# Attention and mixture-of-experts kernel, second phase: another order of the filling work on TensorE

## The chip, the cores and the metric

The kernel runs on one core of one Trainium2 chip. The metric is device time in microseconds (us), as a median of repeated executions. Beside them one execution was taken by the hardware profiler; all durations of single instructions come from it. Five engines work side by side, each in the order of its own queue: TensorE (PE, with weight loads listed apart as PEld), VectorE (DVE), ScalarE (ACT), GpSimd (POOL) and SyncE (SP, which only starts transfers here).

## The reference

The input has 8 rows of 1024 positions with 256 features. Three stages follow one another:

1. An attention within each position over the 64 channels of each of 16 heads, a projection back, a residual and a layer norm.
2. A multi-head attention with 4 heads of 64. Here the first axis (8) is the sequence and the second (1024) the batch, so each position attends over the 8 rows. Then an output projection, a residual and a layer norm, which gives `y1`.
3. A mixture of 8 experts with a capacity, chosen by the largest gate, a residual and two layer norms.

The part that matters for this change is stage 2 and the gates of stage 3:

```python
q, k, v = jnp.split(x @ w.T + b, 3, axis=-1)            # x: (8, 1024, 256)
scores = jnp.einsum('nhld,nhmd->nhlm', q, k) / sqrt(64)  # l, m over the 8 rows
o = jnp.einsum('nhlm,nhmd->nhld', softmax(scores), v)
y1 = ln(x + o @ ow.T + ob) * ln1_g + ln1_b
gates = softmax(y1 @ wg)                                 # 8 experts
```

## The kernel before

The program has three phases, one for each stage. The change lies in the second, `phase_b`.

**Groups.** The 1024 positions are cut into 8 groups of 128. A group `j` holds 128 positions of all 8 rows, 1024 tokens. For the attention the tokens of a group are rearranged into 8 blocks of 128 tokens: 16 positions with their 8 rows each. A block's scores are one 128x128 product, and a bias of -1e30 hides pairs of different positions.

**Steps.** A group is worked in four steps `n` (called parts here). Step `n` treats the feature half `c = n // 2` (two of the four heads) and four blocks, half `ib = n % 2`. Its own work is: `scores` on TensorE with a row maximum on DVE, `weights` (8 exponentials on ACT, in two halves of four), and `normed` on DVE. The step after that transposes the weights (`turn_s` on TensorE, a copy to `sT` on ACT) and multiplies them by the values (`weighted` on TensorE, a copy to `oT` on ACT). So the step before is always completed inside the current one.

**Filling work.** Between these, each step runs a list of filling work written by hand in `fills(j)`. It holds work for the next group (`nxt = j + 1`: `turn_x` transposes its input, `project_qk` and `project_v` make queries, keys and values) and for the group before (`prv = j - 1`: `output`, `normal`, `turn_y`, `logits`, `exps`, `choice`). `put(part, condition, function, arguments)` appends a job to the list of a part. The order of emission is the order in each engine's queue, because the scheduler is switched off (`manual_schedule`): an instruction that waits holds up everything behind it on its engine. The loop places the jobs so: one job after `scores` and before the first four exponentials; two jobs between `turn_s` and the last four exponentials; the rest after `weighted`. In part 0, `some` stops in front of an `output`, as that needs `oT` of the step before.

**What each job puts where.** A pair means two of the 8 rows; `l0` is 0, 2, 4 or 6.

- `turn_x(j, l0)`: four transposes on TensorE, two copies to `xT` on DVE. There is one `xT` buffer. The four calls together fill it, and each `project_qk` reads all rows of it.
- `project_qk(j, c, which, half)`: four 512-wide products on TensorE, one bias on ACT. `which` is 0 for queries and 1 for keys, `half` picks four of the eight blocks. The last one, `(1, 1, 1)`, is first read by the scores of part 3.
- `project_v(j, b0)`: eight products, one addition on DVE.
- `output(j, l0)`: first `xb`, the input plus a bias, on POOL (line 732); four products on TensorE; the sum `r` on DVE (line 750), which reads both; then moments on DVE and the inverse root on POOL (lines 69 to 75).
- `normal(j, l0)`: two scalings on DVE (line 759), a multiplication and an addition on POOL (line 762) that finish `y`, a third operation on POOL (line 763), and a store by SP.
- `turn_y(j, l0)`: four transposes of `y` on TensorE (line 774), a copy to `yT` on ACT.
- `logits(j, l0)`: eight small products on TensorE (line 786), a copy on DVE.
- `expert_bias`: two operations on DVE, over a weight tile that SP loads.

**PSUM.** All filling jobs and `weighted` take their PSUM tile from one pool of three, named `fill`; the scores have a pool of two double tiles, and one tile belongs to the experts:

```python
tc.tile_pool(name="bsc", bufs=2, space=PSUM) as p2,
tc.tile_pool(name="bps", bufs=1, space=PSUM) as p1,
tc.tile_pool(name="bfill", bufs=3, space=PSUM) as pf,
```

The loop that sets where jobs stand among the step's own work:

```python
st = scores(j, c, ib)
some(1)
weights(st, 0)
...
sT = turn_s(before[3])
some(2 if live else 0)
...
weighted(*before[:3], sT)
...
some(len(work))
```

Group `j = -1` only prepares group 0, group 7 has no next group (two experts are computed there instead, as filling), and `j = 8` completes group 7.

Of the kernel before, what the change touches and what calls it, by code (L numbers as in the profile page):

```python
# [38 lines left out]
L, N = 8, 1024  # L39
NT = L * N // P  # L40
NJ = N // P
# [4 lines left out]
EARLY = 2  # L46
# [494 lines left out]
def phase_b(tc, a, ident, x1_d, rows_d, keep, norm_scalars):  # L541
# [8 lines left out]
    with (  # L550
# [315 lines left out]
        def fills(j):  # L866


            o = [[], [], [], []]
            nxt, prv = j + 1, j - 1  # L870
            N = nxt < NJ
            O = prv >= 0
            X = 0 <= j < E - EARLY

            def put(part, ok, fn, *args):
                if ok:
                    o[part].append((fn, *args))

            put(0, N, turn_x, nxt, 0)
            put(0, N, turn_x, nxt, 2)  # L880
            put(0, N, turn_x, nxt, 4)
            put(0, O, output, prv, 0)
            put(0, N, turn_x, nxt, 6)
            put(0, O, output, prv, 2)
            put(0, X, expert_bias, EARLY + j, 0)
            put(0, O, normal, prv, 0)
            put(0, N, project_qk, nxt, 0, 0, 0)
            put(1, O, normal, prv, 2)
            put(1, O, turn_y, prv, 0)
            put(1, O, output, prv, 4)  # L890
            put(1, N, project_qk, nxt, 0, 0, 1)
            put(1, O, logits, prv, 0)
            put(1, O, normal, prv, 4)
            put(1, O, turn_y, prv, 2)
            put(1, X, expert_bias, EARLY + j, 1)
            put(1, N, project_v, nxt, 0)
            put(1, O, logits, prv, 2)
            put(1, N, project_qk, nxt, 0, 1, 0)
            put(2, O, turn_y, prv, 4)
            put(2, O, output, prv, 6)  # L900
            put(2, N, project_qk, nxt, 0, 1, 1)
            put(2, O, logits, prv, 4)
            put(2, O, normal, prv, 6)
            put(2, X, expert_bias, EARLY + j, 2)
            put(2, N, project_v, nxt, 2)
            put(2, N, project_qk, nxt, 1, 0, 0)
            put(2, N, project_v, nxt, 4)
            put(3, O, turn_y, prv, 6)
            put(3, N, project_qk, nxt, 1, 0, 1)
            put(3, N, project_v, nxt, 6)  # L910
            put(3, O, logits, prv, 6)
            put(3, O, exps, prv)
            put(3, X, expert_bias, EARLY + j, 3)
            put(3, N, project_qk, nxt, 1, 1, 0)
            put(3, O, choice, prv)
            put(3, N, project_qk, nxt, 1, 1, 1)
            if j == NJ - 1:
                for n in range(4):
                    for i in range(EARLY):
                        k = EARLY * n + i  # L920
                        put(n, True, expert, *divmod(k, 4))
            return o

        before = None
        for j in range(-1, NJ + 1):
            if j < 0:
                load_x(0)
                load_x(1)
            parts = fills(j)
            for n in range(4):  # L930
                work = list(parts[n])
# [454 lines left out]
```

## Time and profile before

| What | Value |
|---|---|
| Time, median of 3 (lowest to highest) | 5169.2 us (5164.46 to 5169.56) |
| The profiled execution's own time | 5132.98 us |
| Its span, first to last instruction | 5131.2 us |
| Mean granted TensorE clock | 0.980 |
| First phase, up to the first `turn_x` wait's end | 0 to 4356.4 us |
| Group -1 and group 0 of the second phase | 4356.4 to 4426.1 us |
| Groups 1 to 6 | 4426.1 to 4775.9 us |
| Groups 7 and 8 | 4775.9 to 4886.3 us |
| Third phase | 4886.3 to 5131.2 us |

The starts of groups 1 to 7, taken at the first matmul of their scores (line 660), are 4426.11, 4483.68, 4543.64, 4601.84, 4659.94, 4718.00 and 4775.87 us. A group thus takes about 58 us, of 5131 in all. Times in the text are read on this axis; "start to start" is the distance between the first instructions of two neighbouring runs of matmuls on TensorE, because the ends of matmuls are modelled and overlap the next start. A wait in brackets behind an instruction is the idle time of its engine before it and what ended it.

### The profile page before, as it was taken

To read this page: it belongs to the slowest core of one execution; us is meant where nothing else is said; L and a number is where in the kernel's file an instruction comes from. 1 tells how busy PE (TensorE), PEld (TensorE's weight loads), DVE (VectorE), ACT (ScalarE), POOL (GpSimd) and SP (SyncE) were. 2 spreads that over 40 slices of the span, in tenths; PEclk is the share of its full clock that TensorE was granted. 3 is DMA by queue.
4 is the path that set the end of the run, shared out by engine and by line. 5 is a ranking of instruction groups with operands and counts; after the bars stand their busy time and mean duration, and the time that the engine had idled before them with its cause. 6 is when DMAs were issued, how large, how long until landed. Compare 5 with 4: busy or idle time off the path is not lost. (4 is left out here: it accounts for less than half of the span.)

```text
span 5131.2 us, 189707 instructions
## 1 busy us (share of the span) xinstructions
PE 4902.1 (96%) x79688; PEld 3308.8 (64%) x79688; DVE 3068.7 (60%) x6088; ACT 3359.7 (65%) x4123; POOL 3369.5 (66%) x7014
## 2 busy tenths in 40 slices
PE   7999999999999999999999999999999997888775
PEld 4666666666666666666666666666666664566563
DVE  5656656666666666566665666666566663455467
ACT  4777777777777777777777777777777774444334
POOL 5676676767776676776776776776767675245446
PEclk9999999999999999999999999999999998999897
DMA  2222222222221222222222222222222222122253
GB/s 75 47 48 48 48 47 48 49 47 48 48 49 46 48 48 48 49 49 46 48 49 46 49 49 46 48 49 46 48 48 47 48 49 67 47 67 73 70 185 115
DMA packets 575501, 286.30 MB, mean 56 GB/s; under 512 B 395057, under 2 KB 526257, under 8 KB 574641
## 3 DMA queue, kind: packets, MB, share of 16 engines
q1 hardware_dynamic: 366162, 111.51, 11.0%
q0 software_dynamic: 204800, 159.82, 10.5%
q8 instruction: 623, 10.21, 0.9%
q10 hardware_dynamic: 3680, 2.83, 0.2%
q14 instruction: 236, 1.93, 0.1%
HBM read 72.31 MB, written 33.59 MB: 21 GB/s over the span
## 5 line engine op out<-in xcount | busy, mean ns | idle before, releaser
L359 ACT ACTIVATE e<-pair 128x1024 f32<-128x1024 f32 x3072 | 2977.4, 1021 | 1241.5 <-PE pair L343 1241.5
L403 POOL DMA_DIRECT2D nd<-S x4096 | 1949.3, 484 | 603.6 <-DVE S L393 410.1
L343 PE MATMUL pair<-R,L 32*128 32x128 f32 (+1 forms) x32768 | 1607.0, 323 | 3.8 <-POOL event L314 3.7
L393 DVE COPY S<-sum 128x512 f32<-128x512 f32 x1024 | 706.9, 690 | 1470.3 <-PE sum L382 1143.5
L343 PEld LDWEIGHTS pair<-R,L 32*128 32x128 f32 x32768 | 1271.8, 186 | 50.7 <-POOL event L314 5.0
L373 PE MATMUL sum<-e,V 128*32 128x256 f32 x16384 | 1285.8, 385 | 4.9 <-DVE S L393 4.9
L300 POOL DMA_DIRECT2D R<-qm x2048 | 973.7, 483 | 78.0 <-issue 39.5
L382 PE MATMUL sum<-e,V 128*32 128x128 f32 x16384 | 823.8, 273 | 0.0
L382 PEld LDWEIGHTS sum<-e,V 128*32 128x32 f32 x16384 | 533.1, 110 | 352.8 <-issue 1.8
L373 PEld LDWEIGHTS sum<-e,V 128*32 128x32 f32 x16384 | 406.5, 109 | 236.8 <-DVE vT L241 41.8
L331 PE MATMUL pair<-late,sel 32*128 32x256 bf16 (+1 forms) x6144 | 499.3, 313 | 9.6 <-ACT e L359 9.6
L254 DVE COPY V<-vT 32x128 f32<-32x128 f32 x2048 | 457.5, 223 | 28.1
L331 PEld LDWEIGHTS <-sel 32*128 32x128 bf16 x6144 | 155.4, 91 | 460.6 <-issue 445.2
L412 DVE RECIPROCAL att<-nd 128x256 f32<-128x256 f32 x256 | 447.4, 1747 | 7.2 <-DMA nd<-S 3.3
L314 POOL MEMSET event<- 1x1 f32 x256 | 22.6, 88 | 627.1 <-DMA R<-qm 419.7
L223 PE MATMUL ps<-wk,xT 128*128 128x512 f32 x512 | 257.6, 626 | 10.8 <-DMA wk<-in_Wk 10.0
L234 PEld LDWEIGHTS ps<-xT,wv 128*128 128x128 f32 x2048 | 238.2, 191 | 45.1 <-issue 41.8
L234 PE MATMUL ps<-xT,wv 128*128 128x128 f32 x2048 | 262.6, 281 | 1.6 <-DVE qm L267 0.8
L266 PE MATMUL ps<-wq,xT 128*128 128x512 f32 x512 | 257.5, 626 | 6.5 <-DVE k L224 6.5
L443 PE MATMUL ps<-wo,attT 128*128 128x256 f32 x1024 | 256.9, 394 | 0.7 <-ACT attT L426 0.7
L443 PEld LDWEIGHTS ps<-wo,attT 128*128 128x128 f32 x1024 | 185.4, 191 | 63.3 <-issue 41.8
L73 POOL TENSOR_SCALAR ve<-mv 128x1 f32<-128x1 f32 x128 | 37.4, 292 | 270.2 <-DVE mv L71 268.7
(191 smaller groups left out, 3841.3 us busy)
## 6 DMA issues: line engine op xcount, KB each, us to landing
R<-qm POOLq DMA_DIRECT2D x2048, 32.0 KB, 2.1
nd<-S POOLq DMA_DIRECT2D x4096, 16.0 KB, 1.9
L<-k SPq DMA_DIRECT2D x4088, 8.0 KB
rows_d<-yx SPq DMA_DIRECT2D x32, 512.0 KB
xT<-in_xT SPq DMA_DIRECT2D x64, 128.0 KB
xr<-in_x SPq DMA_DIRECT2D x64, 128.0 KB
x_d<-x1o SPq DMA_DIRECT2D x64, 128.0 KB
x<-x_d SPq DMA_DIRECT2D x8, 1024.0 KB
```

The costliest lines, as they stand in the source:

```text
L234: nc.tensor.matmul(ps[:, i * P : (i + 1) * P], w["v"][:, c, ch * P : (ch + 1) * P], xT_of[t][:, c, :], start=c == 0, stop=c == DC - 1,)
L254: nc.vector.tensor_copy(V[32 * aa : 32 * aa + 32, qd % 2, :, qd // 2, :, aa, 0:4], src[32 * qd : 32 * qd + 32, :, ww, :, aa, :],)
L300: moved.append((None, nc.gpsimd.dma_start(R[:, b, s, b, :], q[:, b, s, cols])))
L331: nc.tensor.matmul(bank[u].rearrange("p (n i) -> p n i", i=n)[:, :, 0:32], sel[pr].rearrange("p a j -> p (a j)"), late[pr, None, :].to_bro ...
L343: one = nc.tensor.matmul(bank[u][:, x * 4 * n : (x + 1) * 4 * n].rearrange("p (b i) -> p b i", i=n), Lt[pr, 2 * (h0 + h) + jb].rearrange(" ...
L359: nc.scalar.activation(e, pair[i], AF.Exp)
L373: nc.tensor.matmul(dst[32 * u : 32 * u + 32], Vs[ww][:, 0, h0 + h, u, :], e0[u // 2][:, u % 2, x * 256 : (x + 1) * 256].rearrange("p (b i) ...
L382: nc.tensor.matmul(dst[32 * u : 32 * u + 32, :, 32:], Vs[ww][:, 1, h0 + h, u, :], e1[u // 2][:, u % 2, h * 128 : (h + 1) * 128].rearrange( ...
L393: nc.vector.tensor_copy(S[:, :, 2 * which : 2 * which + 2, :].rearrange("p b h i -> p h b i"), ps.rearrange("p (h b i) -> p h b i", h=2, b=4),
L403: nc.gpsimd.dma_start(tok[:, b, s, h0 * C1 : (h0 + G) * C1], Sx[:, 4 if s else b, b, :])
L412: nc.vector.reciprocal(att[:, cols], nd[:, 1, cols])
L443: nc.tensor.matmul(ps[:, :D], attT[:, c, :], wo[:, c, :], start=c == 0, stop=c == HID // P - 1)
```

## The change

The lists of `fills` are put in another order; no job is added or taken away.

```diff
+            put(0, 0 < j < NJ, project_qk, j, 1, 1, 1)
             put(0, N, turn_x, nxt, 0)
...
             put(0, N, project_qk, nxt, 0, 0, 0)
+            put(1, N, project_qk, nxt, 0, 0, 1)
             put(1, O, normal, prv, 2)
+            put(1, O, output, prv, 4)
             put(1, O, turn_y, prv, 0)
-            put(1, O, output, prv, 4)
-            put(1, N, project_qk, nxt, 0, 0, 1)
+            put(1, X, expert_bias, EARLY + j, 1)
+            put(1, N, project_v, nxt, 0)
             put(1, O, logits, prv, 0)
             put(1, O, normal, prv, 4)
             put(1, O, turn_y, prv, 2)
-            put(1, X, expert_bias, EARLY + j, 1)
-            put(1, N, project_v, nxt, 0)
+            put(1, N, project_qk, nxt, 0, 1, 0)
             put(1, O, logits, prv, 2)
-            put(1, N, project_qk, nxt, 0, 1, 0)
...
-            put(3, N, project_qk, nxt, 1, 1, 1)
+            put(3, j < 0, project_qk, nxt, 1, 1, 1)
```

In part 1, the job between the scores and the exponentials was `normal` of pair 2 and is now a projection. The two behind `turn_s` were `turn_y` of pair 0 and `output` of pair 4 and are now `normal` of pair 2 and `output` of pair 4. `turn_y` of pair 0 comes after `weighted`, followed by `expert_bias` and `project_v`, then `logits` of pair 0. The last projection of a group (keys, second feature half, blocks 4 to 7) leaves part 3 of the group before and becomes the first job of part 0 of its own group, between the scores and the exponentials. For group 0 it stays where it was. In part 0 `turn_x` of pairs 0 and 2 then stand behind `turn_s`, and that of pair 4 behind `weighted`.

## The prediction

> **What bounds the kernel now.** I read three views in this order: the busy time by stretch (to find the second phase and its limit), TensorE's waits in that stretch, then the order of time of each engine for one group of eight rows. The page's busy line and the stretch of groups 1 to 6 come first:
>
> ```profile
> PE 4902.1 (96%) x79688; PEld 3308.8 (64%) x79688; DVE 3068.7 (60%) x6088; ACT 3359.7 (65%) x4123; POOL 3369.5 (66%) x7014
> ...
> 4426.10:4775.90 349.80, 311.25 (x1971) 224.39 (x1972) 206.25 (x460) 152.48 (x510) 165.22 (x192) 0.94 0.27 69
> ```
>
> The columns are the stretch, its length, then busy time of PE, PEld, DVE, ACT and POOL, the granted clock, DMA share and GB/s. TensorE is busy 311 of 350 us there, so it sets the pace; its gaps are all there is to win. The waits of TensorE in this stretch, all of them:
>
> ```profile
> PE fill L774 <- POOL yx L762: 23.2, 6, 3.9
> PE fill L717 <- ACT sT L707: 10.8, 6, 2.1
> PE fill L623 <- DVE xT L612: 3.8, 6, 0.6
> PE fill L742 <- ACT oT L725: 0.8, 5, 0.2
> ```
>
> One wait a group, 3.9 us, for y of the first pair, and one of 1.8 us for sT in part 0. The order of time on TensorE, group 4, part 1 (start, length, engine, line; in brackets the idle time before):
>
> ```profile
> 4616.52 1.09 PE L705 MATMUL sc<-ident,s 128*128 128x128 f32 x8
> 4621.54 1.12 PE L774 MATMUL fill<-ident,yx 128*128 128x128 f32 x4 [3.93 <-POOL yx L762]
> 4622.45 3.62 PE L742 MATMUL fill<-wout,oT 128*128 128x256 f32 x8
> 4626.00 1.41 PE L717 MATMUL fill<-sT,v 128*64 128x128 f32 x16
> 4627.34 1.98 PE L623 MATMUL fill<-xT,wi 128*128 128x512 f32 x4
> 4629.16 0.95 PE L786 MATMUL fill<-wg,yT 128*128 128x8 f32 x8
> ```
>
> After the 3.93 us gap the output product takes 3.55 us from start to start, against 1.73 us in parts 0 and 2. From 4621.54 to 4627.34, 5.80 us hold work that elsewhere takes 0.48 + 1.73 + 1.03 = 3.24. So each such gap costs a further 2.56 us; over groups 1 to 6 this extra is 1.8, 2.8, 2.6, 2.6, 2.5, 2.7, mean 2.5. The chain behind the gap lies on POOL and DVE, same group:
>
> ```profile
> 4620.10 1.39 POOL L762 TENSOR_TENSOR yx<-yx,row_ln_b 128x512 f32<-128x512 f32 x1
> ...
> 4626.51 1.27 POOL L732 TENSOR_TENSOR xb<-x,row_out_b 128x512 f32<-128x512 f32 x1
> ...
> 4627.81 0.69 DVE L750 TENSOR_TENSOR r<-fill,xb 128x512 f32<-128x512 f32 x1 [6.18 <-POOL xb L732]
> ```
>
> y of pair 0 is there at 4621.49. POOL then runs the rest of normal 0, all of normal 2 and only then xb of pair 4, so DVE empties the output product of pair 4 at 4628.50. That last time is the one to keep in mind. Where it already bites is seen in group 7, which has no projections as filling:
>
> ```profile
> 4805.68 0.66 PE L774 MATMUL fill<-ident,yx 128*128 128x128 f32 x4 [1.97 <-DVE r L750]
> ```
>
> Transposes of y have nothing to do with r; what they wait for is the PSUM buffer. The "fill" pool has three; in that part the order is turn_y 0, output 4, weighted, logits 0, turn_y 2, and the fifth waits for the second to be emptied. Buffers go round by three.
>
> **The Trainium skill.** "TensorE: Matmul & The Clock Gate", Part 1, "What's actually happening", says that the array falls to half rate after an idle window and needs about 3.4 us of activity, in a free-running window, to come back. The trace agrees in kind (1.73 becomes 3.55 us); gaps of 1.73 us left the rate alone in five groups, one of 2.13 us (group 2, part 0) did not. "PSUM — Partial Sum Buffer", "Specifications (TRN2)": 8 banks of 512 fp32 values. Pools here take 2x2 (sc) + 1 (pw) + 3 (fill) = 8, so no fourth fill buffer exists. "Perfetto Trace Analysis", "Optimization Strategy": the same gap repeated on the saturated engine can mean that buffers ran out; L774 in group 7 shows just that.
>
> **The change, part by part**, in group 4 (T0 = 4601.84, T1 = 4615.31, T2 = 4634.87 are the starts of parts 0, 1, 2).
>
> *Part 1 reordered.* Nothing is added or removed. New order with TensorE's warm lengths: scores 1.21 (to 4616.52), project_qk 1.82 (18.34), turn_s 0.87 (19.21), output 4 1.73 (20.94), weighted. It waits for sT, which ACT finishes at 4621.55 + 1.02 = 22.57: the row max on DVE, which it hangs on, stays behind the norm of pair 0. ACT does the projection's bias (0.69) before the exponentials, with time to spare. Gap 1.6 us, then weighted to 23.6 and turn_y 0 to 24.1, whose y has been there since 21.49: that wait is gone. Next in TensorE's queue stands project_v 0. Fill buffers now: project_qk, output 4, weighted, turn_y 0, project_v 0. The fifth needs the second empty: r of pair 4, 4628.50. Before, the fifth was logits 0, reached at 4629.16, 0.66 us after the buffer was free; the change puts TensorE there 4.4 us before. Behind the stall wait logits 0, turn_y 2, project_qk and logits 2; all later work follows. POOL's order is unchanged, so 4628.50 does not move by itself.
>
> After it: 1.73 (v) + 0.81 + 0.48 + 1.82 + 0.81 = 5.65 us warm, 0.06 for the release, and the slow rate after a gap of over 3.9 us, 2.5. T2 = 28.50 + 0.06 + 5.65 + 2.5 = 36.71 against 34.87: +1.84. Bounds of the slow rate: 1.0 (a lucky phase) to 2.8, so +0.3 to +2.1. The expert bias and v on DVE change places; the norm of pair 4 comes some 2 us later, so POOL has y of pair 4 near 4637.2; turn_y 4 asks at T2 + 1.21 = 37.9: covered, by 0.7. SP's stores and weight loads keep their order. Six groups: 6 x 1.84 = +11.0.
>
> *Projection held back.* Part 3 is shorter by 1.8 us, part 0 longer by it. It stands ahead of turn_s, and turn_x 4 goes behind weighted. TensorE reaches weighted at T0 - 1.8 + 1.21 + 1.82 + 0.87 + 0.9 = T0 + 3.0; sT came at T0 + 5.34. Whether sT moves up depends on what the row max waits for:
>
> ```profile
> 4603.17 1.23 DVE L680 TENSOR_REDUCE mx<-sc 128x8 f32<-128x1024 f32 x1 [0.54 <-PE sc L671]
> ```
>
> In group 4 it waits 0.54 us for the scores after the choice ended on DVE, so 0.5 us is won. In groups 2, 3 and 5 the max starts as the choice ends (a weight load is late before it), so nothing; group 6 gains 0.25, group 1 (no choice, then bound by the bias of the projection on ACT) 0.7. Sum -1.45. So the moved projection mostly fills the gap it opened. But the gap before weighted becomes 1.5, 2.7, 2.3, 1.8, 2.3, 2.1 us in groups 1 to 6. Group 2, slow before, shows the price of crossing:
>
> ```profile
> 4489.43 1.32 PE L717 MATMUL fill<-sT,v 128*64 128x128 f32 x16 [2.13 <-ACT sT L707]
> 4490.68 3.40 PE L742 MATMUL fill<-wout,oT 128*128 128x256 f32 x8
> ```
>
> There r of pair 0 came 1.2 us later after weighted than in other groups (4.76 against 3.56), and the POOL chain starts there. I count groups 3 and 5 and half of 6: 2.5 x 1.2 = +3.0, between 0 and 6.
>
> *Groups 7 and 8.* In 7, part 0 has its gap cut from 3.04 to 2.35 and everything 0.85 earlier; in part 1 logits 0 becomes the fourth fill and waits for r of pair 4, so logits 0 (0.8 warm, 1.4 slow) stands behind 4805.63 - 0.85 as well as turn_y 2 and logits 2. Net +0.5, between -1 and +2. In 8 output 4 goes under the 8.7 us wait for y, but POOL's chain sets that part's end: 0.
>
> Sum: 11.0 - 1.45 + 3.0 + 0.5 = +13 us. The profiled execution took 5132.98 (span 5131.2): 5146. The timed runs have a median of 5169.2, 36 us above; I carry the difference over unchanged: 5182.
>
> **Rivals.** *Forecast, stall moves to the buffer of output 4*: 5182, own range 5171 to 5190. For it: L774 above, waiting for r. *Faster*: buffers do not bind, only the wait for y goes. Then each group saves 3.93 + 2.55 less the new 1.6 before weighted, 4.9 us, six times 29: 5140. Against it: three buffers and the wait in group 7; it would need POOL to reach xb of pair 4 about 4.4 us sooner, and its order is not touched. It decides as soon as r of pair 4 is out before 4624.1. Chance 0.11. *Near nothing*: the stall is there but the slow rate costs about 1 us, and held-back gaps stay warm: 6 x 0.3 - 1.45 + 0.5, about +1, 5170; with middling values up to 5179. Chance 0.22 for this stretch. *Worse*: all six part-0 gaps go slow and part 1 costs 2.1: 12.6 - 1.45 + 7.2 + 2 = +20: 5189. Chance 0.14. The forecast proper has 0.53.
>
> 0.2% of the time, 10.3 us, is what I take as measurable, so slower begins at 5179.5. The forecast (about 0.47 of its 0.53) and worse give slower 0.61; near nothing and the low edge of the forecast 0.27; faster 0.12 (its rival, and a far edge of near nothing). Range: from 5165 to 5193; it leaves out the faster rival and the ends.
>
> **What would show it.** TensorE's waits for yx gone in groups 1 to 6; in their place project_v (L641) waiting 4.4 us for DVE r L750, six times, and double lengths after it; weighted waiting about 1.6 us more in part 1. Part 0 gaps as listed. I am wrong if L641 does not wait, or if r of pair 4 is emptied before turn_y 0 ends.

## The result, and the profile after

The changed kernel takes 5197.32 us (median of 4, 5194.19 to 5200.45) where the kernel before takes 5166.83 (median of 4, 5157.26 to 5169.56): ratio 1.0059, 95% interval 1.0046 to 1.0073, or 30 us more. The direction was forecast; the size was 2.3 times the 13 us of the sum, and the time lies above the range.

The profiled execution of the changed kernel has a span of 5192.5 us, 61 above that of the kernel before, and 40 of these have nothing to do with the change. The busy time by stretch of the changed kernel shows it (columns as in the prediction; groups 1 to 6, then the third phase):

```profile
4418.87:4796.14 377.27, 325.07 (x1970) 234.44 (x1970) 200.62 (x454) 150.67 (x510) 163.97 (x192) 0.91 0.25 64
...
4907.70:5192.50 284.80, 176.80 (x712) 128.68 (x712) 180.99 (x510) 102.97 (x240) 135.93 (x191) 0.79 0.43 133
```

The third phase, untouched, takes 284.8 us here and 244.9 in the profile before. Both lengths recur below whatever the kernel: 243 to 245 in all profiles from chips where the kernel before takes 5128, 288 in the one from a chip where it takes 5171. What makes the chips differ is not shown. This phase is left out of comparisons of two profiles. The second phase, from the first `turn_x` to the first matmul of the third phase, grew from 529.3 us (4357.05 to 4886.33) to 556.2 (4351.49 to 4907.68): +26.9, close to the measured 30. Groups 1 to 6 carry it, 349.8 before and 377.3 after, at a granted clock of 0.91 against 0.94.

TensorE's waits in groups 1 to 6 of the changed kernel (line, what it waited for, total, times, longest):

```profile
PE fill L641 <- DVE r L750: 25.7, 6, 4.3
PE fill L717 <- ACT sT L707: 19.5, 12, 2.3
PE fill L623 <- DVE xT L612: 3.7, 6, 0.6
PE fill L623 <- ACT yT L778: 3.4, 5, 0.7
```

The wait for y (23.2 us before) is gone, and `project_v` waits for the sum r of pair 4 instead, 4.3 us six times. Line 717, `weighted`, now waits twice a group. The last line was not foreseen. Part 1 of group 3 in order of time, first on TensorE, then the one line of DVE that ends the stall:

```profile
4569.61 1.09 PE L717 MATMUL fill<-sT,v 128*64 128x128 f32 x16 [1.50 <-ACT sT L707]
4570.64 0.66 PE L774 MATMUL fill<-ident,yx 128*128 128x128 f32 x4
4575.56 3.78 PE L641 MATMUL fill<-wi,xT 128*128 128x256 f32 x8 [4.27 <-DVE r L750]
4579.14 1.71 PE L786 MATMUL fill<-wg,yT 128*128 128x8 f32 x8
4580.70 1.09 PE L774 MATMUL fill<-ident,yx 128*128 128x128 f32 x4
4582.47 3.78 PE L623 MATMUL fill<-xT,wi 128*128 128x512 f32 x4 [0.68 <-ACT yT L778]
4586.05 1.44 PE L786 MATMUL fill<-wg,yT 128*128 128x8 f32 x8
```

```profile
4574.82 0.69 DVE L750 TENSOR_TENSOR r<-fill,xb 128x512 f32<-128x512 f32 x1 [6.17 <-POOL xb L732]
```

The transposes of y (L774) start at once behind `weighted`. The stall comes next, and ends as DVE empties the buffer of `output` 4 (4574.82 + 0.69 = 4575.51). Then look at the lengths: `project_v` 3.58 us start to start instead of 1.73, the logits 1.56 instead of 0.81, the projection 3.58 instead of 1.82. The half rate lasts from 4575.56 until after 4586, about 11 us; in the kernel before it lasted about 5.

The granted clock, the column behind the five busy times, says the same without any lengths of matmuls. Two stretches of the changed kernel (groups 3 and 4), then one of the kernel before (group 4):

```profile
4573.40:4587.06 13.66, 10.82 (x30) 7.62 (x30) 5.50 (x13) 1.27 (x2) 8.79 (x10) 0.50 0.16 60
4638.26:4641.67 3.41, 2.88 (x7) 2.35 (x8) 3.27 (x8) 0.00 (x0) 2.01 (x4) 0.50 0.25 92
```

```profile
4619.85:4626.68 6.83, 5.14 (x18) 3.96 (x20) 1.79 (x3) 4.41 (x18) 6.67 (x7) 0.50 0.41 107
```

In groups 1 to 6 of both profiles, and of those of all experiments below, the granted clock is either 1.00 or 0.50, and it changes only at times that lie whole multiples of 3.41 us apart, on a grid that lies elsewhere in every run. So the half rate comes in whole pieces of 3.41 us. Counted by the part in which they begin, part 1 of groups 1 to 6 has 1, 2, 2, 2, 2 and 2 pieces in the kernel before and 3, 4, 4, 1, 5 and 3 in the changed one, whose part 1 is shortest (21.31 us) in group 4 with one piece and longest (25.38) in group 5 with five.

Part lengths over groups 1 to 6, from the starts of the scores:

| | Before | After |
|---|---|---|
| Part 0 | 13.46 to 13.48 (15.08 in group 2) | 14.39 to 15.03 (16.79 in group 2) |
| Part 1 | 19.04 to 19.81, sum 116.9 | 21.31 to 25.38, sum 143.6 |
| Part 2 | 13.40 | 13.40, in two groups 14.8 |
| Part 3 | 11.67 | 9.95 |

### The profile page after: what moved, and what is told of

Its sections match the earlier page's. It is cut to its first block, busy times and chain, and to the rows that moved or that the text cites. A ratio compares the mean times of both kernels' runs of the same rounds, so it can differ in the third digit from the quotient of the medians.

```text
span 5192.5 us, 189702 instructions
## 1 busy us (share of the span) xinstructions
PE 4922.2 (95%) x79688; PEld 3323.9 (64%) x79688; DVE 3064.0 (59%) x6088; ACT 3358.0 (65%) x4123; POOL 3370.5 (65%) x7014
```

## The experiments

Each time stands beside runs of the kernel before on the same chip; its median was 5128.3 to 5128.9 in all jobs but the last (5170.9). The changed kernel itself was not timed again: on a chip where the kernel before takes 5128.5, its ratio of 1.0059 would mean 5159. Differences to the changed kernel are taken from the two ratios, and with the intervals of both they are uncertain by 8 to 10 us. Lines inserted into a kernel shift the line numbers behind them: the transposes of y stand at L774, L777 or L780, the logits at L786, L789, L790 or L792, the sum r at L750, L752 or L753.

**1. Is it POOL that delays r of pair 4?**

```diff
+        def normal_behind(j, l0):
+            G["xb", j, l0 + 2] = residual(j, l0 + 2)
+            normal(j, l0)
...
-            put(1, O, normal, prv, 2)
+            put(1, O, normal_behind, prv, 2)
```

`output` uses this xb if it is there.

> The changed kernel, with the input-plus-bias sum xb of pair 4 run on POOL ahead of normal of pair 2 instead of behind it. Theory (the stall of project_v is the wait for r of pair 4, which POOL delays): r of pair 4 is emptied near T1 + 9.4 instead of T1 + 13.2, the 4.3 us wait of L641 falls under 1 us and with it the half rate after it; part 1 falls from 21.3 to 25.4 us to about 17. Time about 5150, that is some 45 below the changed kernel and below the kernel before too. Rival (the half rate in part 1 comes from its many short products, whatever the stall): 5185 to 5190, the gap gone but the double lengths still there.

5115.03 (5111.64 to 5117.58), ratio 0.9976, interval 0.9966 to 0.9986: 13 below the kernel before and 43 below the changed one, where 45 had been expected. Part 1 takes 15.4 to 16.1 us. TensorE in group 4:

```profile
4609.26 1.09 PE L717 MATMUL fill<-sT,v 128*64 128x128 f32 x16 [1.50 <-ACT sT L707]
...
4611.43 1.99 PE L641 MATMUL fill<-wi,xT 128*128 128x256 f32 x8 [0.49 <-DVE r L752]
4613.26 0.95 PE L792 MATMUL fill<-wg,yT 128*128 128x8 f32 x8
...
4620.91 1.02 PE L780 MATMUL fill<-ident,yx 128*128 128x128 f32 x4 [1.54 <-POOL yx L768]
4621.73 1.91 PE L705 MATMUL sc<-ident,s 128*128 128x128 f32 x8
```

The stall shrank to 0.49 us and all lengths in part 1 are single. POOL's order decided the stall: xb now stands ahead of the three instructions of `normal` for pair 2. The last two lines are part 2: y of pair 4 is now late by 1.5 us, and in groups 4 and 6 the rate falls there as well; part 2 takes 15.0 us in four groups and 16.6 to 16.7 in these two.

**2. Would another buffer do?**

```diff
-            ps = pf.tile([P, 512], FP, name="fill")
+            ps = p1.tile([P, 512], FP, name="pw") if l0 == 4 and j < NJ - 2 else pf.tile(...)
```

> The changed kernel, with the output product of pair 4 put in the experts' PSUM bank, which stands idle in groups 0 to 6, so that nothing in the fill pool waits for r of pair 4. Theory (r of pair 4 also stands ahead of the norm and of the addition of v in DVE's own queue): the wait of L641 goes, but project_qk (L623), now the one that comes round to the buffer of project_v, waits for the addition of v, some 5 us; time within 10 us of the changed kernel, 5190 to 5205. Rival (the buffer alone is the cause): no wait over 1 us in part 1 behind weighted, time near 5140.

5134.66 (5127.06 to 5140.76), ratio 1.0011, interval 1.0003 to 1.0020: 24 below the changed kernel, so outside what the theory gave, and 6 above the kernel before, so not the rival either. TensorE and DVE in group 3:

```profile
4560.91 1.98 PE L623 MATMUL fill<-xT,wi 128*128 128x512 f32 x4 [0.67 <-ACT yT L781]
4565.57 1.07 PE L789 MATMUL fill<-wg,yT 128*128 128x8 f32 x8 [2.68 <-DVE v L648]
```

```profile
4560.76 0.69 DVE L753 TENSOR_TENSOR r<-pw,xb 128x512 f32<-128x512 f32 x1 [6.18 <-POOL xb L732]
...
4564.84 0.68 DVE L648 TENSOR_TENSOR v<-fill,row_in_b_v 128x512 f32<-128x512 f32 x1
```

The wait moved on: r still holds DVE until xb comes, the addition of v stands behind it, and the next user of v's buffer waits. Who that is was foreseen for one group only: in groups 1 to 5 the logits wait, 2.7 us, and in group 6, which has no expert bias, `project_qk`, 4.46 us. So the buffers don't go round strictly by three; which one a tile gets depends on the work around it. I had read the wait for r in group 7 of the kernel before as a fixed round.

**3. Does dense work behind the stall bring the rate back sooner?**

```diff
             put(1, N, project_v, nxt, 0)
+            put(1, N, project_qk, nxt, 0, 1, 0)
             put(1, O, logits, prv, 0)
...
-            put(1, N, project_qk, nxt, 0, 1, 0)
             put(1, O, logits, prv, 2)
```

> The changed kernel, with project_qk of part 1 drawn up directly behind project_v, ahead of logits 0, turn_y 2 and logits 2; the stall of 4.3 us stays. Theory (the rate comes back only within a dense stretch of long products; 8-wide logits, transposes and gaps between them put it off): the double lengths end about 5 us after the stall, part 1 falls from a mean of 23.9 us to about 21.7, time about 13 below the changed kernel, 5184. Rival (the rate comes back by the phase of a free-running window alone, whatever runs): the mean of part 1 stays at 23 to 24.5, time 5193 to 5201.

5147.05 (5141.20 to 5150.16), ratio 1.0035, interval 1.0021 to 1.0049: 12 below the changed kernel. Part 1 has a mean of 22.35 us, 21.6 to 23.0, against 23.9 (21.3 to 25.4). Part 1 came out as the theory had it, and the rival (23 to 24.5 us) did not. The time agrees, but 12 us stand against an uncertainty of 10. The rate also fell a second time in groups 3 and 5, and part 2 paid for it. Group 3:

```profile
4573.26 0.95 PE L786 MATMUL fill<-wg,yT 128*128 128x8 f32 x8
4574.07 0.63 PE L774 MATMUL fill<-ident,yx 128*128 128x128 f32 x4
4575.38 1.29 PE L786 MATMUL fill<-wg,yT 128*128 128x8 f32 x8 [0.68 <-ACT yT L778]
4576.60 0.61 PE L660 MATMUL sc<-other,rep 64*128 64x512 bf16 x2
4577.00 1.92 PE L671 MATMUL sc<-qk 64*128 64x128 f32 x16
```

At 4573.26 the rate is full. Three short groups of work and one gap of 0.68 us later the scores take double. This gap is the only one between.

**4. Each half of the change alone.** Part 1 alone:

```diff
-            put(0, 0 < j < NJ, project_qk, j, 1, 1, 1)
...
-            put(3, j < 0, project_qk, nxt, 1, 1, 1)
+            put(3, N, project_qk, nxt, 1, 1, 1)
```

> Only the new order of part 1; the last projection of a group stays in part 3. Theory (part 1 carries the whole loss, the held-back projection wins some 2 us in six groups): 5195 to 5201, no different from the changed kernel by more than 4. Rival (holding back costs as well, through longer gaps before weighted in part 0): 5186 to 5192.

5161.11 (5157.33 to 5169.53), ratio 1.0063, interval 1.0046 to 1.0079: the whole loss, within the noise. The other half, the kernel before with the held-back projection:

```diff
+            put(0, 0 < j < NJ, project_qk, j, 1, 1, 1)
...
-            put(3, N, project_qk, nxt, 1, 1, 1)
+            put(3, j < 0, project_qk, nxt, 1, 1, 1)
```

> Only the held-back projection; part 1 in the old order. Theory (it fills the gap ahead of weighted in part 0 that its own insertion opens): 0 to 5 us below the kernel before, gaps of 1.3 to 2.3 us ahead of weighted in part 0. Rival (gaps over 2 us turn the rate down): 3 to 8 us above.

5124.60 (5117.53 to 5129.82), ratio 0.9990, interval 0.9983 to 0.9997: some 4 us won. Its gaps ahead of `weighted` in part 0 are 1.3 to 2.7 us, and part 0 with them takes 14.4 to 15.8 us; 13.47 + 1.72 = 15.2 would be the whole weight of the moved projection, which four of the six groups stay below.

**5. What does the half rate cost by itself?** Products of no use fill the stall, so that its length stays and its idleness goes. In the changed kernel:

```diff
+        def keep_warm(j, n):
+            pw = p1.tile([P, 512], FP, name="pw")
+            ...
+            for i in range(n):
+                nc.tensor.matmul(pw, wi[:, 0, 0:P], xT[:, 0, 0:512], start=i == 0, stop=i == n - 1)
...
+            put(1, N and O, keep_warm, nxt, 9)
             put(1, N, project_v, nxt, 0)
```

> The changed kernel, with nine 512-wide products of no use (into the experts' idle bank, from operands that lie ready) ahead of project_v 0 in groups 1 to 6, so that TensorE works through about 3.9 of the 4.3 us of the stall; the stall itself stays, project_v starts when it did. Theory (a stall costs its length and, on top, the half rate behind it, which measures 5 us a group in the changed kernel): the double lengths in part 1 and 2 are gone, part 1 takes 19 to 20 us, the time falls by 25 to 32 against the changed kernel, to within 6 us of the kernel before. Rival (the half rate comes from the short products and transposes in part 1, not from the stall): the double lengths stay, time within 8 us of the changed kernel.

5142.10 (5135.87 to 5145.42), ratio 1.0025, interval 1.0014 to 1.0037, 17 below the changed kernel. I had taken a product at half its length: nine take 7.7 us and overrun the stall by 3.3. But behind them all lengths are single, 5.62 us from `project_v` to the scores, against the 5.65 of the prediction's warm sum. With five in place of nine:

> The changed kernel with five products of no use ahead of project_v 0 in place of nine. Nine took 7.7 us, 0.86 each, and overran the stall by 3.3 us; five take 4.3 us, which is the stall. Theory: part 1 falls from 22.2 us with nine to about 18.8, no double lengths, the time 20 below that of the version with nine, so 4 to 10 below the kernel before. Rival (without the overrun the half rate comes back): part 1 at 21 to 24 us, time 10 or more above the kernel before.

5126.94 (5123.44 to 5130.63), ratio 0.9996, interval 0.9987 to 1.0005: equal to the kernel before, and 32 below the changed kernel. Group 4:

```profile
4623.00 4.46 PE L806 MATMUL pw<-xT,wi 128*128 128x512 f32 x10
4627.44 1.99 PE L641 MATMUL fill<-wi,xT 128*128 128x256 f32 x8
4629.27 0.95 PE L786 MATMUL fill<-wg,yT 128*128 128x8 f32 x8
```

`project_v` starts no sooner than with the bare stall, yet part 1 takes 20.0 us (18.8 in group 6) instead of 23.9. That is the price of the half rate in the changed kernel: 32 us by the times, 28 by the parts of the two profiles. That it equals the whole loss is chance, since the kernel before pays for half rate too, about 15 us by the prediction's reading. So half rate makes up about half of the loss. Most of the rest is waiting: 4.27 and 1.50 us a group in the changed kernel in place of 3.93.

**6. Does only idle time count?** The same stall, filled with 21 products that are 8 wide:

```diff
-                nc.tensor.matmul(pw, wi[:, 0, 0:P], xT[:, 0, 0:512], start=i == 0, stop=i == n - 1)
+                nc.tensor.matmul(pw[:, 0:E], wi[:, 0, 0:P], xT[:, 0, 0:E], start=i == 0, stop=i == n - 1)
```

> The changed kernel with the stall filled by 21 products that are 8 wide in place of five that are 512 wide: the same 4.3 us of TensorE at 0.2 us a product, no idle time, but little in the array. Theory (what counts for the rate is how full the array is over some microseconds, and short products count as idle): the double lengths come back behind it, part 1 at 22 to 25 us, time 20 to 35 above the kernel before, as with the bare stall. Rival (only idle time counts): part 1 near 20.0 and the time within 6 of the kernel before, as with the five long products.

5192.28 (5187.29 to 5193.69), ratio 1.0040, interval 1.0026 to 1.0054: 21 above the kernel before (5170.87 on this chip). Part 1 takes 22.1 to 24.2 us. Group 2:

```profile
4509.02 5.14 PE L806 MATMUL pw<-xT,wi 128*128 128x8 f32 x42
4514.01 3.76 PE L641 MATMUL fill<-wi,xT 128*128 128x256 f32 x8
4517.57 1.71 PE L786 MATMUL fill<-wg,yT 128*128 128x8 f32 x8
```

TensorE was not idle for a moment behind `turn_y`, and `project_v` still takes double. The filling took 4.6 to 6.1 us, and in five of the six groups the granted clock fell to 0.50 while it still ran. From `project_v` to the scores the profile has 7.5 to 10.3 us, mean 8.8, where the nine long products left 5.6: 3.2 us a group for the rate. The bare stall cost 5.0, with 20 half-rate pieces in part 1 against 14 here. So idle time is not what counts alone: short products did not hold the rate up. Whether they did a little better than no work at all, or the grid only lay better, is not shown.

**7. The same filling in the kernel before**, ahead of `turn_y` of pair 0: eight products, then four.

> The kernel before, with eight such products of no use in its 3.9 us gap ahead of turn_y 0 in groups 1 to 6. Theory (the half rate costs 2.5 us a group there): 13 to 17 us below the kernel before. Rival (half rate of no weight, other waits take its place): within 5 us of it.

> The kernel before with four products of no use ahead of turn_y 0 in place of eight. Eight took 6.9 us in a gap of 3.9; four take 3.4 us and fit. Theory (2.5 us of half rate a group): part 1 falls from 19.5 us to about 17.1, the time to 12 to 16 below the kernel before. Rival: within 4 us of it.

Eight: 5135.51 (5130.90 to 5143.26), ratio 1.0016, interval 1.0009 to 1.0023, 7 to 8 us slower where 13 to 17 faster was expected; they overran the gap as the nine did, and part 1 takes 20.1 to 20.4 us, all at full rate. Four: 5150.22 (5148.19 to 5158.00), ratio 1.0045, interval 1.0029 to 1.0062, 21 us slower where 12 to 16 faster was expected. Group 4 with four:

```profile
4631.87 0.66 PE L774 MATMUL fill<-ident,yx 128*128 128x128 f32 x4 [0.49 <-POOL yx L762]
...
4638.90 1.06 PE L790 MATMUL fill<-wg,yT 128*128 128x8 f32 x8 [1.71 <-DVE r L750]
4639.81 0.63 PE L774 MATMUL fill<-ident,yx 128*128 128x128 f32 x4
4641.54 3.68 PE L641 MATMUL fill<-wi,xT 128*128 128x256 f32 x8 [1.09 <-DVE lg L799]
```

The half rate behind the first gap is gone, as meant. So TensorE comes to the logits sooner and meets the buffer of r there, 1.71 us; then 0.9 us of logits, 0.6 of transposes, 1.09 of gap, 4.3 us in all without one long product, and `project_v` is at half rate. The kernel before shows neither of these waits: there TensorE came later, because of the rate lost behind the first gap.

**8. A version that beats both.** As in 1, and xb of pair 6 early as well, and in part 2:

```diff
-            put(1, O, normal, prv, 4)
+            put(1, O, normal_behind, prv, 4)
...
-            put(2, O, turn_y, prv, 4)
             put(2, O, output, prv, 6)
             put(2, N, project_qk, nxt, 0, 1, 1)
+            put(2, O, turn_y, prv, 4)
```

> The version with xb of pair 4 ahead of normal of pair 2, and now xb of pair 6 ahead of normal of pair 4, and in part 2 the order output 6, project_qk, turn_y 4 instead of turn_y 4, output 6, project_qk. Theory (part 2 took 15.0 to 16.7 us there because turn_y 4 waited 1.5 us for POOL and the rate fell): part 2 back at about 13.4, six times 2 us, so some 25 us below the kernel before (5103 where that takes 5128). Rival (the wait only moves to r of pair 6 or to weighted): 10 to 16 us below it, as before this edit.

5100.94 (5099.52 to 5104.15), ratio 0.9950, interval 0.9933 to 0.9966: 26 below the kernel before. Part 2 is back at 13.6 us, and in groups 1 to 6 the granted clock is 1.00 throughout. Which of the two further edits did how much was not tried. Last, three filling jobs instead of two behind `turn_s` in part 0:

```diff
-                    some(2 if live else 0)
+                    some((3 if n == 0 else 2) if live else 0)
```

> The best version so far (xb of pairs 4 and 6 early, part 2 in another order), with three filling jobs in place of two behind turn_s in part 0, so that turn_x 4 too stands ahead of weighted. Theory (in part 0 TensorE waits 1.3 to 2.8 us for sT, and the copies of turn_x 4 then stand ahead of the norm on DVE): 0.5 to 1 us less in part 0 of six groups, no gap over 2.1 us but one, 3 to 8 us below the best version, some 5095 where the kernel before takes 5128. Rival (the copies on DVE hold up the norm and with it r of pair 0, and so POOL): no gain or a loss of up to 4.

5099.48 (5094.29 to 5101.25), ratio 0.9945, interval 0.9928 to 0.9961. The gaps ahead of `weighted` in part 0 fall to 0.9 to 1.7 us; the 2 or 3 us that it may have won over the version above, of 3 to 8 expected, lie within the intervals.

## Why the prediction was right in kind and wrong in size

- *The stall moves to r of pair 4*: right. `project_v` waits 4.27 to 4.28 us, foreseen 4.4; item 1 shows that POOL's order makes it, item 2 that DVE's queue would pass it on without the buffer. The prediction found the buffer by "buffers go round by three", which item 2 does not bear out: for `project_v` this gave the right buffer by luck; for the next `project_qk`, which waits for yT and not for v, it would have given the wrong one.
- *T2 = 28.50 + 0.06 + 5.65 + 2.5*: this is the step that failed, by its last term, with 1.0 to 2.8 as its bounds. From `project_v` to the scores of part 2 the profile has 8.1 to 12.1 us, mean 10.75. Less 5.65 of full-rate work and 0.57 for the wait for yT that I had not seen, 4.5 us are left for the rate, and in two groups it reached into part 2 for another 1.4: 5.0 us a group instead of 2.5. I had carried the price over from the kernel before, where a dense output product and `weighted` follow the gap. Here one long product follows, and then 8-wide logits, transposes and a gap. In the record of the granted clock the price is 20 pieces of half rate in part 1 instead of 11; the prediction's bounds allowed for luck with the phase, but only around the two pieces of the kernel before. Item 5 (five long products) puts the whole of it at 32 us, give or take 8. Items 3 and 6 point to what runs behind and in the gap as the reason, and the grid has its share, since the same work in group 4 had one piece. How the price divides between the two stays open.
- The account in the profiles: part 1 of six groups grew by 26.7 us and part 2 by 2.8, where 11.0 had been worked out. Of the 18.5 missing, 15 are six times 2.5 us of rate and 3.4 the waits for yT. The time that the sum started from held: 5166.83 us for the kernel before, where 5169.2 had been carried over.
- *Held-back projection, -1.45 and +3.0*: the gaps came as 1.33, 2.27, 1.97, 1.70, 1.73 and 1.88 us (1.5, 2.7, 2.3, 1.8, 2.3, 2.1 foreseen), and only group 2 turned slow. Part 0 grew by 8.3 us and part 3 shrank by 10.3: -2.0, not +1.6. Alone it wins 4 us.
- *Groups 7 and 8, +0.5*: 110.5 us before and 111.5 after, less the 1.7 us of projection that moved in: -0.6. The reading behind it failed: in part 1 of group 7 `weighted` waits 3.48 us for sT, and the wait for r of pair 4 is 0.27 us and stands before turn_y 2, not before the logits.
- *Worse than the forecast* (5189) had the right sign of the risk but looked for it in part 0 and capped part 1 at 2.1 us a group.
- *Faster* fell with the first wait line. *Near nothing* fell with the half rate.

## What to carry to other kernels

When a wait is removed, look up who empties the PSUM buffer that the next job will take, and follow that back through each engine's queue; here one addition on POOL, moved ahead of three others, was worth 43 us. Do not carry the price of a gap on TensorE over from another place: ask what runs behind it, and put the densest products there. In items 3 and 7, short products with waits between them did what one gap does. Ask the profile for the granted clock of the stretch: it shows the half rate directly.

## What the hardware showed that was not expected

- Short matmuls did not hold the rate up. 42 matmul instructions of 8 columns in 5.0 us, without idle time, were followed by `project_v` at 3.56 us; ten of 512 columns in 4.4 us by the same at 1.83.
- The rate fell without a long gap: 4.3 us of logits, transposes and two gaps of 1.71 and 1.09 us were enough (item 7), and in item 3 a gap of 0.68 us between short work.
- The half rate was granted in pieces of 3.41 us on a fixed grid, and the effect of a gap went with where it lay on this grid as well as with its length. Ahead of `weighted` in part 0, a gap of 1.90 us turned the rate down (item 1, group 2: part 0 at 16.55 us) and one of 3.01 us did not (item 6, group 5: 16.09 us, which is the 14.40 of group 1 with its gap of 1.33, and the longer gap). The first, from 4478.83 to 4480.73, lies whole between two points of its run's grid (4477.69 and 4481.10); the second, from 4675.70 to 4678.71, is cut into 1.36 and 1.65 us by the point at 4677.06. The points are counted from the times at which the granted clock changes. There are 84 such gaps in groups 1 to 6 of the 14 profiles. Take of each the longest share between two points: none of the 62 with 1.65 us or less turned the rate down, though ten of them were over 2 us long in all; all five with 2.03 us or more did, and four of the 17 between.
- It stayed down over about 11 us of work where this is loose (group 3 of the changed kernel: four pieces, the first of which begins within the stall), and over about 5 where it is dense (the kernel before: two pieces).
- The third phase takes 243 to 245 us on some chips and 285 to 288 on others, in kernels that have the same code there.
